# A planner that charges turns of the engines at a shared PSUM bank, with new durations for five kinds of work

## The chip, the cores and the metric

The kernel runs on one core of a Trainium2 chip. A core has five engines that run their own instruction streams: TensorE (PE) multiplies matrices and writes PSUM, VectorE (DVE) and ScalarE (ACT) work element by element, GpSimd (POOL) here issues indirect DMAs and does a few small vector steps, and SyncE (SP) issues the other DMAs. The metric is the device time in microseconds (us) of one execution; the median of three runs is compared. Times from the trace come from one profiled execution.

## The reference

Eight blocks of 512 tokens with 128 features (float32) pass through three layers, each added to its input:

```python
x = x + 0.5 * _L0_ffn_ref(_layernorm(x), ...)
x = x + _L0_attn_ref(_layernorm(x), ...)
x = x + 0.5 * _L0_ffn_ref(_layernorm(x), ...)
```

The feed-forward layer (FFN) normalizes each token, finds the nearest of 8 centroids, and sends the token through that expert alone: an up matrix of 128 x 512, `a * silu(g)` of its halves, and a down matrix of 256 x 128. The attention layer is a linear recurrence over the 512 tokens of a block. It projects r, k and v, takes sigmoid of r and exp of k, scans `kv` and `k` with a decay of its own for each channel, divides the two scans, multiplies by r, and projects with W_o.

## The kernel before

**Tables and pairs.** Tokens of one expert are brought together through tables in HBM. For each block, routing finds the expert and the slot of each token; ACT scales the rows (`xrow`, L442), and POOL scatters them with an indirect DMA into a table t (L706, 128 rows each, four for a block). Tiles of 128 slots are then gathered from the table by SP (`xg`, L856), with the weights of their expert (`wup`, L863). There are three tables: one for blocks 0 to 3 and one for blocks 4 to 7 in the first FFN, and one for all blocks in the second, which is filled in the batches (0,1), (2,3), (4,5), (6), (7). Unused slots of a table are filled with zeros by SP.

Two tiles make a pair; 44 pairs are numbered through: 0 to 11 and 12 to 23 in the first FFN, 24 to 43 in the second. A pair goes through these steps, in `pair`: transpose on PE into the x half of `ps_xy` (L869); copy to SBUF as `xgT`, mostly on ACT (L897); up, 16 passes on PE (L874); SILU on ACT into `sg` (L906); product on DVE (L911); down on PE into the y half of `ps_xy` (L882); `ys` on DVE, which adds the skip row (L918); and an indirect DMA for each tile on POOL that puts the rows back to the tokens' places (L924). `xg` holds seven pairs, `sg` three, `ys` four. Both halves of `ps_xy` are one PSUM bank. Another bank, `ps_small`, has scores of routing in one part ("d") and ranks in another ("r").

**Between the FFNs.** Attention works on the batches in turn: statistics (L470), a root on ACT and a newton step on POOL (L505 to L508), scaling and transposes, products for k, r and v on PE (L983), then `kv`, two scans and the divisions on DVE (L998 to L1010), and the output product on PE (L1033 to L1040). The results are the x of the second FFN, whose routing follows: statistics, roots, transposes (L517), scores (L612), nearest centroid (L629 to L663), ranks (L679 to L690), and places of tiles (L745 to L772). The first four pairs of the second FFN, 24 to 27, use tiles that are already full and are worked on beside attention.

**The order.** The steps are not issued as they are written. They are recorded as `Op`s in a `Plan`, with the buffers that each reads and writes (`Buf`), one or more ways (an engine, an estimated duration and a call), an order key by engine, and a lag. `schedule` is a list scheduler: it keeps for each engine when it is free, for each tag of buffers when a slot comes free, takes the op that could start first, and among those on the same engine that could start within `slack` the one with the lowest key. A release costs `HOP` = 0.1, an ACT table load `SWITCH` = 1.28. `trace` runs it with 48 settings of its three parameters and emits the calls in the order of the setting with the least planned span. Each engine then runs its own stream in that order, and waits by semaphores. The keys of a pair k on PE are `LATE + 10k - 13` for the transpose, `LATE + 10k` for up, and `LATE + 10k + 10` for down; the pair's steps on ACT and DVE go ahead of others (`FIRST + k`).

An op's buffer in `ps_xy` is a `Buf` with the tag "x" or "y", each with one slot. The schedule before knows nothing of two tags in one bank. The kernel as built, however, has waits between accesses to one bank by different engines.

Of the kernel before, what the change touches and what calls it, by code (L numbers as in the profile page):

```python
# [19 lines left out]
class Buf:  # L20


    def __init__(self, make, tag=None):
        self.make, self.tag, self.tile = make, tag, None
        self.writers, self.readers = [], []

    def __call__(self):
# [5 lines left out]
class Op:  # L33
    def __init__(self, ways, reads, writes, order, lag, table):
        self.ways, self.order, self.lag, self.table = ways, order, lag, table
        self.bufs = list(dict.fromkeys(list(reads) + list(writes)))
        self.needs, self.users = set(), []


class Plan:  # L40

# [13 lines left out]
    def add(self, ways, reads=(), writes=(), order=None, part=False, lag=0.0, table=None):  # L57
        op = Op(ways, reads, writes, order or {}, lag, table)
        for b in reads:
            op.needs.update(b.writers)  # L60
            b.readers.append(op)
        for b in writes:
            op.needs.update(b.readers)
            if not (part and not b.readers):
                op.needs.update(b.writers)
            if b.readers or not part:
                b.readers, b.writers = [], []
            b.writers.append(op)
        op.needs.discard(op)
        self.ops.append(op)  # L70

    def schedule(self, spare, wait, slack):

        left, ready, uses = {}, {}, {}
        for op in self.ops:
            left[op], ready[op] = len(op.needs), 0.0
            for b in op.bufs:
                uses[b] = uses.get(b, 0) + 1
        slots = {tag: [0.0] * n for tag, n in self.slots.items()}
        free, held, released, table = {}, set(), {}, None  # L80
        waiting = [op for op in self.ops if not op.needs]
        order, span = [], 0.0
        while waiting:
            could = []
            for op in waiting:
                at = ready[op]
                for b in op.bufs:
                    if b.tag and b not in held:
                        if not slots[b.tag]:
                            break  # L90
                        at = max(at, min(slots[b.tag]))
                else:
                    for n, (engine, cost, call) in enumerate(op.ways):
                        then = max(at, free.get(engine, 0.0))
                        if n == 0 or free.get(op.ways[0][0], 0.0) > then + spare:
                            if op.table not in (None, table):
                                then += wait
                            could.append((then, engine, cost, call, op))
            if not could:
                return None  # L100
            first = min(could, key=lambda c: c[0])
            start, engine, cost, call, op = min(
                (c for c in could if c[1] == first[1] and c[0] <= first[0] + slack),
                key=lambda c: (c[4].order.get(c[1], c[4].index), c[0]),
            )
            load = None
            if op.table not in (None, table):
                load = table = op.table
                cost += max(0.0, self.SWITCH - wait)
            order.append((op, call, load))  # L110
            for b in op.bufs:
                if b.tag and b not in held:
                    slots[b.tag].remove(min(slots[b.tag]))
                    held.add(b)
            waiting.remove(op)
            free[engine] = start + cost
            end = start + cost + op.lag
            span = max(span, end)
            for b in op.bufs:
                uses[b] -= 1  # L120
                released[b] = max(released.get(b, 0.0), end)
                if uses[b] == 0 and b.tag:
                    slots[b.tag].append(released[b] + self.HOP)
            for u in op.users:
                left[u] -= 1
                ready[u] = max(ready[u], end + self.HOP)
                if left[u] == 0:
                    waiting.append(u)
        return span, order
# [20 lines left out]
def kernel(  # L150
# [40 lines left out]
    P = 128  # L191
# [99 lines left out]
    ps_xy = ps_t.tile([P, 2 * (P + D)], F32, tag="xy", name="ps_xy")  # L291
# [13 lines left out]
    def part_of(bank, tag, at, width, count):  # L305

        slots[tag], n = count, [0]

        def make():
            first = at + n[0] % count * width  # L310
            n[0] += 1
            return bank[:, first : first + width]

        return lambda: Buf(make, tag)

    small_d = part_of(ps_small, "d", 0, TMAX * E, 128 // (TMAX * E))
    small_r = part_of(ps_small, "r", 128, E * (TMAX + 1), RBUF)
# [1 line left out]
    add = plan.add  # L319
    FIRST, LATE = -10**6, 10**6  # L320
    EXP, SILU = "natural_log_exp_and_others", "silu_and_others"
    x_ = [Buf(lambda b=b: xb[b]) for b in range(B)]
    wd_, wr_, wo_, routing_, attending_ = (Buf(lambda w=w: w) for w in (wsb, wrkv_sb, wo_sb, None, None))
# [139 lines left out]
    def moments(batch, n: str, mv):  # L463

        T = len(batch) * NT
        bn = buf(stat, [P, TMAX, 2, 3], F32, "bn", n, 4)

        def stats(i, b):
            for t in range(NT):
                nc.vector.bn_stats(  # L470
                    bn()[:, i * NT + t, :, :].rearrange("p a m -> p (a m)"), xb[b][:, t, :]
                )

        def aggregate():


            a, o = bn()[:, :T, 0, :], bn()[:, :T, 1, :]
            d = o[:, :, 0]
            nc.vector.tensor_tensor(
                mv()[:, :, :T].rearrange("p m t -> p t m"), a[:, :, 1:], o[:, :, 1:], ALU.add  # L480
            )
            nc.vector.tensor_sub(d, a[:, :, 1], o[:, :, 1])
            nc.vector.scalar_tensor_tensor(d, d, D / 4.0, d, ALU.mult, ALU.mult)
            nc.vector.tensor_add(mv()[:, 1, :T], mv()[:, 1, :T], d)

        for i, b in enumerate(batch):
            add([("DVE", 1.1, lambda i=i, b=b: stats(i, b))], [x_[b]], [bn], part=True)
        add([("DVE", 0.66, aggregate)], [bn], [mv, bn])

    def roots(n, va, rs, part, shape):  # L490
# [79 lines left out]
    def prepare(table, batch, near):  # L570

        f = table.f
        n = f"{f}_{batch[0]}"
# [30 lines left out]
        ps_d = small_d()  # L604
        rows = []
        for i, b in enumerate(batch):
            ps = side(f"x_{f}_{b}")
            xT = buf(work, [P, L], F32, "xT", f"{f}_{b}", 2)

            def products(i=i, xT=xT):  # L610
                for t in range(NT):
                    nc.tensor.matmul(  # L612
                        ps_d()[:, ts(i * NT + t, E)], xT()[:, ts(t, P)], cw, start=True, stop=True
                    )

            add([("PE", 0.5, lambda ps=ps, b=b: transposed(ps, x_[b]))], [x_[b]], [ps], lag=0.2)
            add(copied(xT, ps, L, 0.6, 0.68), [ps], [xT])
            add([("PE", 1.75, products)], [xT, routing_], [ps_d], lag=0.2, part=True)
            row = Buf(lambda b=b: xrow[b][:, :, :D])
            half = Buf(lambda b=b: xrow[b][:, :, D : 2 * D])  # L620
            at = i * NT
            add(scaled(x_[b], row, lambda at=at: rs()[:, 1, at : at + NT],
                       lambda at=at: nra()[:, 1, at : at + NT]), [x_[b], rs, nra], [row])
            add(scaled(x_[b], half, lambda at=at: one()[:, at : at + NT],
                       lambda at=at: nra()[:, 0, at : at + NT]), [x_[b], one, nra], [half])
            rows.append([row, half])
# [210 lines left out]
    def pair(k, table, parts, keep, spots, at_, downs, downs_, tiles):  # L837
        n = len(tiles)
        early = table.left > 0
        xg = buf(work, [P, 2, ROW], F32, "xg", k, 7)  # L840
        wup = buf(work, [P, 2, H2], F32, "wup", k, WUP)
        slots["x"] = slots["y"] = 1
        ps_x = Buf(lambda: ps_xy[:, : 2 * P], "x")
        xgT = buf(work, [P, 2 * P], F32, "xgT", k, 3)
        hp = buf(ps_t, [P, 2, H2], F32, "h", k, 2)
        sg = buf(work, [P, 2, H], F32, "sg", k, 3)
        ps_y = Buf(lambda: ps_xy[:, 2 * P :], "y")
        y = buf(work, [P, 2, D], F32, "ys", k, 4)
        soon = {"ACT": FIRST + k, "DVE": FIRST + k}

# [36 lines left out]
        for i, j in enumerate(tiles):  # L887
            add([("SP", 0.52, lambda i=i, j=j: rows(i, j))], [at_] + parts, [xg], {"SP": LATE + k},
                part=True, lag=2.3)
        for i, j in enumerate(tiles):  # L890
            add([("SP", 0.52, lambda i=i, j=j: weights(i, j))], [at_], [wup], {"SP": LATE + k},
                part=True, lag=3.8)
        add([("PE", 0.19 * n, features_first)], [xg], [ps_x],
            {"PE": LATE + 10 * k - 13}, lag=0.2)
        add(
            [
# [4 lines left out]
            ],  # L901
            [ps_x, cols_], [xgT], soon,
        )
        add([("PE", 0.95 * n, up)], [xgT, wup], [hp], {"PE": LATE + 10 * k}, lag=0.2)
        add(
            [("ACT", 0.16 + 0.22 * n, lambda: nc.scalar.activation(  # L906
                sg()[:, :n, :], hp()[:, :n, H:], AF.Silu))],
# [4 lines left out]
                sg()[:, :n, :], hp()[:, :n, :H], sg()[:, :n, :]))],  # L912
            [hp, sg], [sg], soon,
        )
        add([("PE", 0.53 * n, down)], [sg, downs_, wd_], [ps_y], {"PE": LATE + 10 * k + 10}, lag=0.2)

        half = lambda: ps_y()[:, : n * D].rearrange("p (i d) -> p i d", d=D)
        add([("DVE", 0.1 + 0.18 * n, lambda: nc.vector.scalar_tensor_tensor(  # L918
# [180 lines left out]
```

## Time and profile before

| | us |
|---|---|
| runs | 352.85, 346.55, 344.47; median 346.55 |
| profiled execution, its time | 316.78 |
| its span | 314.0 |
| PE busy | 231.9 (74%) |
| DVE busy | 179.6 (57%) |
| ACT busy | 163.1 (52%) |
| POOL busy | 177.2 (56%) |
| mean granted clock of PE | 0.899 |

Times in the trace count from the start of the span. In rows of instructions, `out<-in` gives the program's names of the tiles, followed by the number of instructions, busy time, mean duration in ns, and the idle time of the engine just ahead of them with what ended it. A wait "A <- B: total, times, longest" is idle time of A that ended when B did. Line numbers are those of the kernel before; in the kernel after, most lines are 8 further down.

### The profile page before, as it was taken

The page shows a single profiled execution, that of the slowest core. Times are in us where ns is not written, and L with a number is a line of the kernel's source. Part 1 is how long each engine was busy: PE and PEld are TensorE (multiplying, and loading weights), DVE is VectorE, ACT ScalarE, POOL GpSimd, SP SyncE. Part 2 cuts the span into 40 slices and gives each one's busy share as a digit, 9 for nine tenths or more (in the row PEclk, how much of TensorE's full clock was granted, in tenths as well). Part 3 has the DMA queues.
Part 4 walks back from the last instruction along what each step waited for, and adds up shares of the span by engine and source line. Part 5 has one row for each costly group of instructions (what it writes and reads, how often), then busy time and mean ns, then how long its engine had stood idle before and what let it go on. Part 6 is the DMA issues. An engine that isn't in the chain of part 4 may idle for free. (4 is left out here: it accounts for less than half of the span.)

```text
span 314.0 us, 5775 instructions
## 1 busy us (share of the span) xinstructions
PE 231.9 (74%) x1510; PEld 194.2 (62%) x1510; DVE 179.6 (57%) x604; ACT 163.1 (52%) x331; POOL 177.2 (56%) x258
## 2 busy tenths in 40 slices
PE   3747467789997889997969368799670186989980
PEld 2636356778897786766736222579470075989980
DVE  4677936314232474898888648999774703242340
ACT  3779951432332359983638565766875233324320
POOL 6268737777564475564446767015377623556663
PEclk9999999999999999997957559999965569999996
DMA  7912569998987996300024154520063488899810
GB/s 211 276 53 85 194 190 336 283 384 260 286 262 229 300 342 200 120 13 10 9 71 134 51 165 187 140 67 25 20 204 145 135 251 268 269 281 324 265 56 10
DMA packets 45138, 55.81 MB, mean 178 GB/s; under 512 B 6255, under 2 KB 31115, under 8 KB 45106
## 3 DMA queue, kind: packets, MB, share of 16 engines
q1 hardware_dynamic: 39286, 42.71, 45.3%
q0 software_dynamic: 5792, 12.73, 11.2%
q8 instruction: 12, 0.20, 0.3%
q14 instruction: 20, 0.16, 0.2%
q10 hardware_dynamic: 28, 0.01, 0.0%
HBM read 39.11 MB, written 17.68 MB: 181 GB/s over the span
## 5 line engine op out<-in xcount | busy, mean ns | idle before, releaser
L874 PE MATMUL h<-xgT,wup 128*128 128x128 f32 x680 | 87.9, 285 | 0.0
L874 PEld LDWEIGHTS h<-xgT,wup 128*128 128x128 f32 x680 | 84.6, 202 | 1.4 <-issue 1.4
L706 POOL DMA_INDIRECT t<-xrow,posi_t x64 | 65.1, 1017 | 30.3 <-issue 15.9
L924 POOL DMA_INDIRECT yt<-ys,xg x46 | 53.1, 1155 | 39.7 <-DVE ys L918 25.6
L924 POOL DMA_INDIRECT out_dram<-ys,xg x39 | 39.5, 1012 | 50.1 <-DVE ys L918 31.1
L911 DVE TENSOR_TENSOR sg<-h,sg 128x512 f32<-128x512 f32 (+1 forms) x44 | 29.1, 671 | 62.5 <-ACT sg L906 62.5
L882 PE MATMUL ps_xy<-wsb,sg 128*128 x340 | 48.2, 286 | 9.7 <-DVE sg L911 5.3
L897 ACT ACTIVATE xgT<-ps_xy,cols 128x256 f32<-128x256 f32 (+1 forms) x44 | 20.5, 465 | 61.2 <-DVE ys L918 33.5
L882 PEld LDWEIGHTS ps_xy<-wsb,sg 128*128 128x128 f32 x340 | 43.2, 198 | 12.8 <-ACT xgT L897 4.7
L906 ACT ACTIVATE sg<-h 128x512 f32<-128x512 f32 (+1 forms) x44 | 25.1, 582 | 37.3 <-PE h L874 37.2
L442 ACT ACTIVATE xrow<-x,nra,rs 128x128 f32<-128x128 f32 x64 | 26.3, 481 | 15.1 <-DVE nra L594 15.1
L612 PE MATMUL ps_small<-cw,xT 128*128 128x8 f32 x128 | 23.9, 319 | 11.4 <-ACT xT L459 6.5
L612 PEld LDWEIGHTS ps_small<-cw,xT 128*128 128x128 f32 x128 | 23.3, 275 | 14.0 <-ACT xT L459 12.7
L869 PE MATMUL ps_xy<-ident,xg 128*128 128x128 f32 x85 | 21.3, 308 | 13.4 <-DMA xg<-t 12.4
L918 DVE SCALAR_TENSOR_TENSOR ys<-ps_xy,xg 128x256 f32<-128x256 f32 (+1 forms) x44 | 18.1, 411 | 18.8 <-PE ps_xy L869 8.7
L442 ACT ACTIVATE xrow<-x,nra,one 128x128 f32<-128x128 f32 x64 | 26.1, 479 | 0.0
L869 PEld LDWEIGHTS ps_xy<-ident,xg 128*128 128x128 f32 x85 | 11.9, 150 | 20.2 <-DMA xg<-t 14.5
L144 ACT ACT_TABLE_LOAD x16 | 20.5, 1283 | 0.3
L679 PE MATMUL ps_small<-onehot_t,tri 128*128 128x32 f16 (+1 forms) x11 | 2.2, 196 | 20.0 <-DVE near L629 8.2
L470 DVE BATCH_NORM_STATS2 bn_f<-x 128x6 f32<-128x128 f32 x64 | 13.5, 277 | 4.3 <-DMA x<-in_L_attn_inputs_dram 3.8
L682 PEld LDWEIGHTS <-ones_h 128*128 128x128 f16 x11 | 1.1, 103 | 21.8 <-issue 21.8
L517 PE MATMUL side_x<-ident,x 128*128 128x128 f32 x64 | 13.1, 356 | 1.8 <-ACT x L459 1.4
(156 smaller groups left out, 319.1 us busy)
## 6 DMA issues: line engine op xcount, KB each, us to landing
wup<-in_L_ffn_up_w_dram SPq DMA_DIRECT2D x85, 256.0 KB
xg<-t SPq DMA_DIRECT2D x85, 130.0 KB
t<-fill SPq DMA_DIRECT2D x27, 130.0 KB
x<-in_L_attn_inputs_dram SPq DMA_DIRECT2D x8, 256.0 KB
x<-yt SPq DMA_DIRECT2D x8, 256.0 KB
wsb<-in_L_ffn_down_w_dram SPq DMA_DIRECT2D x8, 128.0 KB
t<-xrow,posi_t POOLq DMA_INDIRECT x64
yt<-ys,xg POOLq DMA_INDIRECT x46
```

Of the source, the lines that this page charges most:

```text
L144: self.load_table(load)
L442: nc.scalar.activation(out()[:, t, :], src()[:, t, :], AF.Identity, bias=bias()[:, t : t + 1], scale=scale()[:, t : t + 1],)
L612: nc.tensor.matmul(ps_d()[:, ts(i * NT + t, E)], xT()[:, ts(t, P)], cw, start=True, stop=True)
L706: ordered(table, nc.gpsimd.indirect_dma_start(out=table.at()[:, :], out_offset=bass.IndirectOffsetOnAxis(ap=posi()[:, q : q + 1], axis=0), ...
L869: nc.tensor.transpose(ps_x()[:, ts(i, P)], xg()[:, i, :D], ident)
L874: nc.tensor.matmul(hp()[:, i, ts(c, P)], wup()[:, i, ts(c, P)], xgT()[:, ts(i, P)], start=True, stop=True,)
L882: nc.tensor.matmul(ps_y()[:, ts(i, D)], sg()[:, i, ts(c, P)], wdown[c][:, ds(expert(downs[j]) * W, D)], start=(c == 0), stop=(c == NHC - 1),)
L897: ("ACT", 0.2 + 0.13 * n, lambda: nc.scalar.activation(xgT()[:, : n * P], ps_x()[:, : n * P], AF.Copy, scale=scale_c)),
L906: [("ACT", 0.16 + 0.22 * n, lambda: nc.scalar.activation(sg()[:, :n, :], hp()[:, :n, H:], AF.Silu))],
L911: [("DVE", 0.1 + 0.28 * n, lambda: nc.vector.tensor_mul(sg()[:, :n, :], hp()[:, :n, :H], sg()[:, :n, :]))],
L918: add([("DVE", 0.1 + 0.18 * n, lambda: nc.vector.scalar_tensor_tensor(y()[:, :n, :], half(), 0.5, xg()[:, :n, D : 2 * D], ALU.mult, ALU.ad ...
L924: inst = nc.gpsimd.indirect_dma_start(out=table.result()[:, :], out_offset=bass.IndirectOffsetOnAxis(ap=xg()[:, i, 2 * D : 2 * D + 1].bitc ...
```

## The change

A `Buf` may now name its bank: both parts of `ps_small` are in bank "small", both halves of `ps_xy` in bank "xy". For each bank, `schedule` keeps when each engine's last planned access ends, and starts an op on the bank no earlier than `HOP` after the end of every other engine's last access. Accesses by the same engine are not held. And five duration estimates are changed: statistics of one block on DVE 1.1 to 0.9, scores of one block on PE 1.75 to 1.5, the pair's transpose 0.19 to 0.17 a tile, up 0.95 to 0.9 a tile, down 0.53 to 0.5 a tile. The computation of each op is untouched.

```diff
-    def __init__(self, make, tag=None):
-        self.make, self.tag, self.tile = make, tag, None
+    def __init__(self, make, tag=None, bank=None):
+        self.make, self.tag, self.bank, self.tile = make, tag, bank, None
...
+        self.banks = {b.bank for b in self.bufs if b.bank}
...
                         then = max(at, free.get(engine, 0.0))
+                        for bank in op.banks:
+                            for other, end in banks.get(bank, {}).items():
+                                if other != engine:
+                                    then = max(then, end + self.HOP)
...
             end = start + cost + op.lag
+            for bank in op.banks:
+                banks.setdefault(bank, {})[engine] = end
...
-        return lambda: Buf(make, tag)
+        return lambda: Buf(make, tag, "small")
...
-            add([("DVE", 1.1, lambda i=i, b=b: stats(i, b))], [x_[b]], [bn], part=True)
+            add([("DVE", 0.9, lambda i=i, b=b: stats(i, b))], [x_[b]], [bn], part=True)
...
-            add([("PE", 1.75, products)], [xT, routing_], [ps_d], lag=0.2, part=True)
+            add([("PE", 1.5, products)], [xT, routing_], [ps_d], lag=0.2, part=True)
...
-        ps_x = Buf(lambda: ps_xy[:, : 2 * P], "x")
+        ps_x = Buf(lambda: ps_xy[:, : 2 * P], "x", "xy")
...
-        ps_y = Buf(lambda: ps_xy[:, 2 * P :], "y")
+        ps_y = Buf(lambda: ps_xy[:, 2 * P :], "y", "xy")
...
-        add([("PE", 0.19 * n, features_first)], [xg], [ps_x],
+        add([("PE", 0.17 * n, features_first)], [xg], [ps_x],
...
-        add([("PE", 0.95 * n, up)], [xgT, wup], [hp], {"PE": LATE + 10 * k}, lag=0.2)
+        add([("PE", 0.9 * n, up)], [xgT, wup], [hp], {"PE": LATE + 10 * k}, lag=0.2)
...
-        add([("PE", 0.53 * n, down)], [sg, downs_, wd_], [ps_y], {"PE": LATE + 10 * k + 10}, lag=0.2)
+        add([("PE", 0.5 * n, down)], [sg, downs_, wd_], [ps_y], {"PE": LATE + 10 * k + 10}, lag=0.2)
```

More of the change, by code (lines that the diff above doesn't have):

```diff
@@ L79, in schedule @@
         slots = {tag: [0.0] * n for tag, n in self.slots.items()}
-        free, held, released, table = {}, set(), {}, None
+        free, held, released, table, banks = {}, set(), {}, None, {}
         waiting = [op for op in self.ops if not op.needs]
```

## The prediction

> **What bounds the kernel now.** I read the page's rows and slices first, then the list of waits, then timelines of the stretches where the order moves most. No engine is full, and the limit changes by stage:
>
> ```profile
> PE   3747467789997889997969368799670186989980
> PEclk9999999999999999997957559999965569999996
> DMA  7912569998987996300024154520063488899810
> ```
>
> Each digit is a fortieth of 314.0 us, 7.85 us. Slices 8 to 15 (60 to 117 us) are pairs of the first FFN: PE and DMA both near full. Slices 33 to 39 are the last pairs. Between them DMA is nearly idle, and PE drops to half clock around 229.8 to 257.1 us: there the kernel waits for a chain that goes through several engines. That chain is where an order can cost or gain.
>
> The waits show where PSUM turns already stand:
>
> ```profile
> ACT xgT L897 <- DVE ys L918: 33.5, 23, 4.1
> POOL out_dram L924 <- DVE ys L918: 31.1, 10, 15.6
> SPq L856 <- DMA t<-xrow,posi_t: 23.3, 6, 10.7
> ```
>
> Columns: total us, times, longest us. The first is the turn that the change charges: the x half of the pair bank is read by ACT only after DVE has read the y half, although the halves are different buffers. Each such wait (mean 33.5/23 = 1.46 us) is on ACT while PE is in its 16 passes, so most cost nothing: a steady pair takes about 3.36 us, PE needs 0.38 + 1.95 + 1.06 = 3.39 minus overlaps (about 2.9), and DMA is 0.94 busy in 60 to 117 us. The other two rows are the gap before pair 28: POOL idle for 15.6 us until ys of pair 24, and SP waiting 10.7 us for scatters. The timeline of POOL in it:
>
> ```profile
> 211.06 1.19 POOL L924 DMA_INDIRECT out_dram<-ys,xg  x1 [15.64 <-DVE ys L918]
> 216.54 1.39 POOL L924 DMA_INDIRECT out_dram<-ys,xg  x1 [2.99 <-DVE va L588]
> 225.35 1.01 POOL L924 DMA_INDIRECT out_dram<-ys,xg  x1 [4.56 <-DVE slot_t L690]
> 227.95 0.97 POOL L706 DMA_INDIRECT t<-xrow,posi_t  x1 [0.30 <-ACT x L459]
> 243.82 0.96 POOL L706 DMA_INDIRECT t<-xrow,posi_t  x1 [1.06 <-ACT xrow L442]
> 245.09 0.96 POOL L706 DMA_INDIRECT t<-xrow,posi_t  x1 [0.30 <-ACT xrow L442]
> ```
>
> From 225.35 POOL is full, a DMA each 1.27 us (0.97 and 0.30 of issue). SP gathers xg_28 only when the first two scatters of xrow_6 (started 243.82 and 245.09) have landed: it issues at 247.65, 2.56 after the second starts. Then:
>
> ```profile
> 249.95 1.05 PE L869 MATMUL ps_xy<-ident,xg 128*128 128x128 f32 x2 [3.58 <-DMA xg<-t]
> 253.34 3.62 PE L874 MATMUL h<-xgT,wup 128*128 128x128 f32 x16
> ```
>
> So from the last step of attention on batches 4 and 5 (num_4 final on DVE, ends 205.54; call it N4) POOL's queue sets when the 16 last pairs start, 42.1 us later.
>
> **What the change does to the work.** No instruction's arithmetic changes. The new durations lie by their rows: bn_stats, four of 0.21, 0.86 against 0.9; products 23.9/16 = 1.49 against 1.5; transposes 0.38 for two tiles against 0.34; up 1.8 between starts against 1.8; down 1.06 against 1.0. They and the bank turns only choose another order. Three things differ in count: ACT table loads 16 to 18, one copy (xT_0_7) goes from ACT to DVE, one scaling of batch 7 from DVE to ACT as four instructions. I follow the built order of both through the stages, placing each instruction by the durations of its row.
>
> *Start to the first pair (0 to 50 us).* Two rank matmuls of the first table go ahead of later products and places for its tiles come about 1.6 us earlier; but nra_0_4 falls behind on DVE, so the rows of blocks 4 to 7 are scaled to about 48.5 instead of 43.95, and PE's registers for the second table are read ahead of UP of pair 1. Between -3 (all the earlier places) and +2; I take -0.5, because the gather waits for scatters on POOL, whose number is unchanged.
>
> *First FFN (50 to 117 us).* The same pattern (transpose k+1, UP k, down k-1) to pair 12. Then in three places UP and down are two pairs apart, each with a turn of the bank ahead of it of 1.1 to 1.2 us. Against it, the layer-norm statistics of batch 0, which stop DVE for 3.25 us until the block is loaded (and PE for 1.59 + 0.73 behind it), come a pair later: up to -2. With DMA at 0.94, 0, from -2 to +2.
>
> *Attention of batches 0 to 3 with pairs 19 to 23 (117 to 164 us).* The last five pairs now come ahead of the key/receptance/value products of these batches. DVE binds it (33.1 of 40 us busy in 117 to 157); no operation is added, but attention's DVE work starts later by the pairs put before it: +1 by what the places of their DVE instructions move, +3.6 if all of it shows. The earlier loads of blocks 4 to 7 help only a stage that is not bound by them. I take +1.5.
>
> *To N4 (164 to 205 us).* The scaling and keys of batches 4 and 5 go ahead of the row scaling of blocks 2 and 3 on ACT (6.26 us of it in one run), and two newtons ahead of scatters on POOL; but er_4 stays behind these rows, and the two side banks then hold up the value product. From -2.5 to +1.5; I take -0.5. N4 comes +0.5 later.
>
> *N4 to the gather of pair 28.* This is the step that decides. In the order before, on PE down of pair 24 comes ahead of the output product of batch 6; after, behind it and behind the transposes of batch 6. On DVE ys_24 has nine instructions after N4 ahead of it before (4.8 us: 205.54 to 210.36). After, it is behind three scans, the rest of batches 6 and 7, all statistics of batches 4 to 6 and the whole nearest-centroid chain to onehot8_t2_4. By rows: 5 of 0.68 and 3 of 0.75 (L1005), 3 scans of 1.22, 2 sg of 0.67, kv 0.65, statistics 3 x 0.86 and 8 x 0.17, va, nra and one 0.8, near and argmin 1.76: 17.8, and 0.5 for a wait on the scores' matmuls: ys_24 starts at N4 + 18.3. Out scatters of pair 24 stand at the head of POOL's queue, as before, and start 0.7 after ys_24 does: N4 + 19.0 in place of N4 + 5.5. In front of xrow_6's second scatter stand then 2 + 3 + 1 + 1 + 2 + 1 + 2 + 1 + 3 + 1 = 17 DMAs and two newtons (1.1 each by the rows of 237.79 on): it starts at N4 + 19.0 + 17 x 1.27 + 2.2 = N4 + 42.8, and with 2.56 to the issue xg_28 is at N4 + 45.4, against 42.1 before: +3.3, and 0.2 for what POOL still waits on its way (8.6 in three waits before). Between +0 (DVE gets there earlier, because parts of batches 6 and 7 are done before N4) and +8 (the scatters also wait for rows of 6 and 7, whose scaling ACT does late). I take +3.5, the sum by rows.
>
> Queued behind are also the two new table loads, on ACT around sg_26, sg_27 and the roots of batches 6 and 7. The row:
>
> ```profile
> L144 ACT ACT_TABLE_LOAD x16 | 20.5, 1283 | 0.3
> ```
>
> The Trainium skill's "ScalarE: Activation LUTs", section "What ACT_TABLE_LOAD costs", says that a switch is 1283 ns and about 1380 of drain, 2.66 in all. The row has 1283, but idle of 0.3 for all 16 together, and the first instruction after the load starts 0.01 later: no drain shows here. By the row the two are 2 x 1.283 = 2.6 us, by the page 5.3. At POOL's pace of 17 DMAs behind them, 2.6 is covered; 5.3 would put roots of 7 behind their scatter and show about 1. I take 0, between 0 and +2.6.
>
> *Pairs 28 to 43 (254 to 314 us).* The SILU table is loaded right after the second pair's xgT instead of after the third's, so sg of pair 28 follows its UP at once: before, PE waited 1.74 us. Against it xg_30's second tile is behind zero fills on SP, xg_31 behind weights that wait for UP of 28. From -2 to +1; I take -0.5.
>
> The "PSUM — Partial Sum Buffer" page of the same skill, section "PSUM bank collisions raise a hardware error", speaks for a charge: two engines may not touch one bank in the same part at once, whatever the address. The 33.5 us row is what a program pays for that. By the rule, 23 turns are worth up to 33.5 us if avoided; by the row they lie under UP, and the pair stage's PE idle for them is L882 behind ACT and DVE, 6.8 + 4.6 us in all of the run, most outside 60 to 104. I therefore count no general gain.
>
> **Sum.** -0.5 + 0 + 1.5 - 0.5 + 3.5 + 0 - 0.5 = +3.5; the clock adds 0.5 if one more transpose falls at half speed (0.48 against 0.19 a tile), so +4. On the profiled execution: 316.78 (314.0 span and 2.78 around it) + 4 = 320.8. The median of the runs shown is 346.55, 29.8 above that execution, and the page doesn't say where those lie; I add the 4 as such: 350.55, said 350.5.
>
> **Rivals.**
> *Faster.* The pairs and attention take the cover away from three stalls: 3.25 (statistics of batch 0), 3.58 (DVE for the value product at 125.05), 1.28 (the load at 257.86), in all 8.1, and DVE reaches ys_24 early enough that POOL is not later. 346.5 - 8.1 = 338.4. For it: all three are gone from their place. Against: DVE binds there, and POOL's gap is 15.64 already.
> *Same.* The stages are bound by DMA and by busy DVE, which do not change; the turns were paid by both orders, so the new charge only reshuffles: 346.5, within 2 either way. It is also the case that the change doesn't do what it says. For it: every total of work is unchanged. Against: ys_24's place.
> *Slower by over 2%.* The one mechanism is the late ys_24 at POOL's head: with attention's +3.6 and pushing scatters to the +8 bound, 346.5 + 11.5 = 358. It decides from about 7 us more in the gap. For it: POOL is in order and full afterwards; its cover (8.6 us of waits before) is used up.
>
> **Chances.** Forecast (+1.5 to +7) 0.50, the same 0.15, slower 0.25, faster 0.10. 2% is 6.9 us, and the three runs before spread 344.47 to 352.85, so that is about what can be told from no change. Part of the forecast, near its top, may read over the bound: slower 0.29, same 0.61, faster 0.10. The range that leaves out 2 in 10 goes from 342 to 360.
>
> **What would show it.** In the trace after: POOL idle in one piece of over 20 us before the first out_dram scatter of the second half, ys_24 some 18 us after N4, no idle on POOL behind it, and xg_28 issued 45 to 46 us after N4; N4 itself within 3 us of 205.5; 18 table loads and their idle still near 0.3; steady pairs at 3.3 to 3.4. The prediction is wrong if N4 moves by more than 4 us, or if PE's waits for bank turns in 60 to 117 us fall by more than 3.

## The result, and the profile after

The kernel after took 360.51 us (median of 4 runs, 356.21 to 361.15) where the kernel before, measured with it, took 347.27 (344.47 to 352.85). The ratio is 1.035, 95% interval 1.029 to 1.041. It is slower by more than 2%; the prediction had 350.5 and gave that case 0.29. A ratio leaves out the runs that are over 1.5% above the fastest of the same kernel, and a median takes all runs, so the two can differ.

The two kernels took 347 and 361 us in this first measurement and 321 and 327 us in all later ones, on four chips; the pages don't show why, and the chip of the first is not known. The profile of before that the prediction was read from (316.78) fits the later level, and the profile of after from the first measurement (361.15, span 359.4) does not. So I compare traces and medians within like conditions: before (314.0, and 320.0 for a second trace) against the kernel after run again (325.2 and 325.8).

The slices of the page of after, first measurement, in the same rows as before (a slice is 9.0 us):

```profile
PE   3568206777885879797939765599772177967880
PEclk9999555599999889999867877879685578999996
DMA  8723657787767698410400153420252558877610
```

The half-clock stretch around the gather of pair 28 is there again (slices 30 and 31 counted from 0, 270 to 288 us; the gather is at 280.93), and there is another in slices 4 to 7, 36 to 72 us, up to the first ys at 71.61. Work in total is nearly the same: 1510 matmuls, 604 instructions on VectorE, 258 on GpSimd, and 336 in place of 331 on ScalarE. The table loads of the same page:

```profile
L152 ACT ACT_TABLE_LOAD x18 | 23.1, 1283 | 0.3
```

18 of the same 1283 ns with 0.3 of idle in all, as the prediction took them: no drain shows. The waits that answer to those shown of before, from the trace of after run again (325.2):

```profile
ACT xgT L905 <- DVE ys L926: 7.0, 5, 2.5
POOL tr L513 <- ACT yr L505: 34.0, 2, 20.0
SPq L864 <- DMA t<-xrow,posi_t: 24.5, 8, 12.9
```

The bank's turns, ACT's xgT behind DVE's ys, fall from 33.5 us to 7.0. The order pays fewer turns; the time went elsewhere. (The charge is not what removes them: with the new durations and no charge, in the run dur_only below, this wait is 6.5 us, and with the charge and the old durations, in bank_only, 26.1.) GpSimd's longest wait is now 20.0 us, for the roots of batches 4 and 5 in the routing of the second FFN. And there is a part of GpSimd's timeline (first measurement) that no row shown of before resembles:

```profile
211.03 2.31 POOL L714 DMA_INDIRECT t<-xrow,posi_t  x1 [0.30 <-issue]
213.36 1.11 POOL L513 TENSOR_TENSOR tr_a<-van,yr_a 128x4 f32<-128x4 f32 x1
214.54 2.06 POOL L514 TENSOR_TENSOR tr_a<-tr_a,yr_a 128x4 f32<-128x4 f32 x1
216.69 1.10 POOL L515 TENSOR_TENSOR tr_a<-three_halves,tr_a 128x4 f32<-128x4 f32 x1
217.87 1.11 POOL L516 TENSOR_TENSOR rn<-tr_a,yr_a 128x4 f32<-128x4 f32 x1
219.13 1.00 POOL L714 DMA_INDIRECT t<-xrow,posi_t  x1 [0.15 <-issue]
```

This is the newton step of batch 7 in attention: 4 small instructions on 128 x 4 numbers, 5.6 us from start to end. In a trace of before the same four take 1.1. The columns are start, duration, engine, line, operation. Beside it, VectorE in the same trace:

```profile
213.13 1.28 DVE L1013 SCALAR_TENSOR_TENSOR den<-kT,gam,den 128x1024 f32<-128x1024 f32 x1
214.33 2.28 DVE L1018 TENSOR_TENSOR_SCAN num<-lam_l,kv 128x1024 f32<-128x1024 f32 x1
216.53 1.20 DVE L1013 SCALAR_TENSOR_TENSOR den<-den,er 128x1024 f32<-128x1024 f32 x1
217.65 1.28 DVE L1013 SCALAR_TENSOR_TENSOR num<-kv,gam,num 128x1024 f32<-128x1024 f32 x1
```

VectorE's four end at 214.41, 216.61, 217.73 and 218.93; GpSimd's four end at 214.47, 216.60, 217.79 and 218.98. Each of GpSimd's instructions ends with one of VectorE's. The profile that the prediction was read from has the same on a smaller scale: a newton step of 0.55 us, where the others take 0.20, beside an instruction of VectorE that ends 0.05 us before it:

```profile
176.71 0.55 POOL L507 TENSOR_TENSOR tr_a<-three_halves,tr_a 128x4 f32<-128x4 f32 x1
176.53 0.68 DVE L966 TENSOR_TENSOR xl<-x,rn 128x512 f32<-128x512 f32 x1
```

And ScalarE waits for what they make (first measurement again):

```profile
213.01 0.59 ACT L467 COPY xlT<-side_xl 128x512 f32<-128x512 f32 x1 [0.60 <-PE side_xl L525]
219.01 1.27 ACT L980 ACTIVATE xl<-x,rn 128x128 f32<-128x128 f32 x4 [5.42 <-POOL rn L516]
220.20 0.67 ACT L999 ACTIVATE kT<-side_k,acols 128x512 f32<-128x512 f32 x1
```

That xl of batch 7 is the scaling that the change moved from VectorE to ScalarE. It now holds ScalarE for 5.42 us, with keys of batch 6 and the reciprocals of batches 4 and 5 queued behind it. GpSimd's queue did not bring the step late: it starts at 213.36, and ScalarE comes free at 213.60.

### The profile page after: what moved, and what is told of

Its sections match the earlier page's. It is cut to its first block, busy times and chain, and to the rows that moved or that the text cites. A ratio compares the mean times of both kernels' runs of the same rounds, so it can differ in the third digit from the quotient of the medians.

```text
span 359.4 us, 5761 instructions
## 1 busy us (share of the span) xinstructions
PE 244.8 (68%) x1510; PEld 201.7 (56%) x1510; DVE 181.1 (50%) x604; ACT 165.4 (46%) x336; POOL 176.8 (49%) x258
## 5 line engine op out<-in xcount | busy, mean ns | idle before, releaser
L882 PE MATMUL h<-xgT,wup 128*128 128x128 f32 x680 | 94.0, 298 | 5.6 <-ACT xgT L905 5.0
L882 PEld LDWEIGHTS h<-xgT,wup 128*128 128x128 f32 x680 | 90.0, 213 | 6.7 <-ACT xgT L905 5.7
L714 POOL DMA_INDIRECT t<-xrow,posi_t x64 | 64.3, 1005 | 37.6 <-issue 19.6
L932 POOL DMA_INDIRECT yt<-ys,xg x46 | 48.2, 1048 | 53.4 <-DVE ys L926 36.7
L919 DVE TENSOR_TENSOR sg<-h,sg 128x512 f32<-128x512 f32 (+1 forms) x44 | 29.5, 669 | 81.3 <-ACT sg L914 61.6
L932 POOL DMA_INDIRECT out_dram<-ys,xg x39 | 38.5, 987 | 45.3 <-DVE ys L926 30.4
L890 PE MATMUL ps_xy<-wsb,sg 128*128 x340 | 49.3, 290 | 12.4 <-DVE ys L926 12.4
L890 PEld LDWEIGHTS ps_xy<-wsb,sg 128*128 128x128 f32 x340 | 44.5, 203 | 16.9 <-DVE ys L926 14.9
L450 ACT ACTIVATE xrow<-x,nra,one 128x128 f32<-128x128 f32 x64 | 26.1, 480 | 0.0
L620 PEld LDWEIGHTS ps_small<-cw,xT 128*128 128x128 f32 x128 | 21.3, 255 | 5.7 <-issue 2.8
L620 PE MATMUL ps_small<-cw,xT 128*128 128x8 f32 x128 | 21.6, 301 | 2.9 <-issue 1.9
L152 ACT ACT_TABLE_LOAD x18 | 23.1, 1283 | 0.3
L513 POOL TENSOR_TENSOR tr<-va,yr 128x8 f32<-128x8 f32 (+1 forms) x11 | 2.8, 256 | 37.6 <-ACT yr L505 33.3
L1048 PEld LDWEIGHTS side_o<-wo_sb,num 128*128 128x128 f32 x64 | 10.6, 237 | 10.4 <-DVE num L1013 6.5
```

Of the source, the lines that this page charges most:

```text
L152: self.load_table(load)
L450: nc.scalar.activation(out()[:, t, :], src()[:, t, :], AF.Identity, bias=bias()[:, t : t + 1], scale=scale()[:, t : t + 1],)
L620: nc.tensor.matmul(ps_d()[:, ts(i * NT + t, E)], xT()[:, ts(t, P)], cw, start=True, stop=True)
L714: ordered(table, nc.gpsimd.indirect_dma_start(out=table.at()[:, :], out_offset=bass.IndirectOffsetOnAxis(ap=posi()[:, q : q + 1], axis=0), ...
L882: nc.tensor.matmul(hp()[:, i, ts(c, P)], wup()[:, i, ts(c, P)], xgT()[:, ts(i, P)], start=True, stop=True,)
L890: nc.tensor.matmul(ps_y()[:, ts(i, D)], sg()[:, i, ts(c, P)], wdown[c][:, ds(expert(downs[j]) * W, D)], start=(c == 0), stop=(c == NHC - 1),)
```

## Where the time went, stage by stage

From the traces in like conditions (means of two: before 314.0 and 320.0, after 325.2 and 325.8), worked out from the starts of instructions; N4 is the end of the last division of batches 4 and 5:

| stage | before | after | difference | forecast |
|---|---|---|---|---|
| start to ys of pair 0 | 60.6 | 60.8 | +0.2 | -0.5 |
| to the last division of batches 2 and 3 | 101.2 | 107.2 | +6.0 | +1.5 |
| to N4 | 44.1 | 42.5 | -1.6 | -0.5 |
| N4 to the gather of pair 28 | 44.7 | 48.9 | +4.3 | +3.5 |
| gather to ys of pair 28 | 14.8 | 12.9 | -1.9 | -0.5 with the next |
| to ys of pair 43, and the end | 51.7 | 53.2 | +1.5 | |

The forecast's remaining +0.5 is its term for the clock, which it gave to no stage. The sum is +8.5 between spans; the medians say +6.0 and +5.7. Two traces of one kernel differ by up to 5.1 us in a row (before, N4 to the gather: 42.1 and 47.2), so a row alone proves little.

Pairs 19 to 23 end 11 us earlier (ys of pair 23 at 147.9 against 158.9), as their place in the order foretold, and attention of blocks 0 to 3 pays it back: the first scatter of the second FFN starts at 174.8 and 176.3 against 166.4 and 168.0, and pair 24 is gathered at 208.2 and 209.3 against 197.2 and 200.2.

## The experiments

My first theory was the prediction's: ys of pair 24 late, at the head of GpSimd's queue, so the gap before pair 28 is longer. All kernels below do the same operations in another order, some of them on another engine. Times are medians; both kernels spread by 3 to 4% within a measurement, so I read medians taken together against each other and give the ratio with its interval beside them. The edits are shown in part; `...` stands for lines left out, and a comment for the lines that do what it says.

**A second trace of before.**

```diff
(no edit)
```

> The kernel before, unedited, for a second trace. Its profiled execution took 316.78 us where its timed runs took 344 to 353, while the kernel after took 361.15 in its profiled execution and 356 to 361 in its timed runs: the two traces at hand may not be alike. If the 30 us are in the execution and not in the kernel, a new profile reads 340 to 352 us, and has stalls that the first lacks: a first ys near 70 us instead of 59.7, and pairs of 4 us instead of 3.4. If the first profile is the rule for a profiled execution, it reads 314 to 320 again, and then the kernel after lost 45 us by its order alone.

321.97 us, span 320.0. The first profile of before was no oddity: under these conditions the kernel takes about 320, timed (321.03) or profiled. Neither case of the expectation was quite met (314 to 320, or 340 to 352). The second is the nearer in its number, but what it concluded, a loss of 45 us by the order, does not follow: the 30 us lie in the conditions of the first measurement. What they consist of the pages don't show.

**The kernel after in these conditions.**

```diff
(no edit)
```

> The kernel after, unedited, in the conditions in which the kernel before has its profile near 316 to 322 us. Theory (the order itself costs the 3.5%): 1.03 to 1.04 times the kernel before, near 332 us, with its trace later than before's by some 4 us at the first pair and 4 to 8 us in the gap before pair 28. Rival (the loss belongs to the conditions of the first measurement, in which gathers and completions came late, and this order only bears them worse): within 1% of the kernel before, near 321 us.

326.61 against 320.6; ratio 1.018, interval 1.003 to 1.033. Between the two cases. The loss is the order's own, but 6 us here and 13 in the first measurement; the two intervals just touch. What makes it larger in the first stays open, as there is no trace of before at that level. A later measurement, with six runs of after, gave 326.76 against 321.02 without a ratio:

> The kernel after's order, unedited, beside the three others in the same call: ratio to the kernel before 1.01 to 1.035, as the two measurements so far (1.018 and 1.035) leave it. If it comes at 1.03 while the conditions are those of the 320 us of before, the loss is the order's; if at 1.018 or less, the first measurement's surplus belongs to its conditions.

The same 1.8%, by medians.

**Parts of the change.** The durations alone, the charge alone, and the new durations with the charge for one bank:

```diff
 dur_only:   -  return lambda: Buf(make, tag, "small")    +  return lambda: Buf(make, tag)
             -  ps_x = Buf(..., "x", "xy"), ps_y alike    +  ps_x = Buf(..., "x"), ps_y alike
 bank_only:     the five durations as before
 xy_only:    -  return lambda: Buf(make, tag, "small")    +  return lambda: Buf(make, tag)
 small_only: -  ps_x = Buf(..., "x", "xy"), ps_y alike    +  ps_x = Buf(..., "x"), ps_y alike
```

> The five new durations, and no charge for a bank. Theory (it is the charge that puts the steps of pairs 24 to 27 behind attention): within 2% of the kernel before, 341 to 353 us. Rival (any change of the planner's numbers reshuffles the order of all stages, and the order before was a lucky one): 354 to 366 us, like the kernel after.

> The charge for turns at a bank, with the five old durations. Theory (the charge is the cause): 354 to 366 us, like the kernel after, with ys of pair 24 more than 12 us behind the last division of batches 4 and 5. Rival (the durations, or the reshuffle as such): anywhere from 341 to 366, with ys of pair 24 within 8 us of that division if it is as fast as before.

> New durations, and the charge at the pair bank alone (x and y halves of ps_xy), not at the routing bank. Theory (the pair bank's charge holds down of pair 24 back): 354 to 362 us, ys of pair 24 late. Rival (the routing bank's charge, which orders scores and ranks, is what moves the starts of the FFNs): within 2% of before, 341 to 353 us.

> New durations, and the charge at the routing bank alone. Theory (both charges together are what puts pair 24's steps behind attention): near the kernel before, 314 to 322 us, ys of pair 24 within 8 us of the last division of batches 4 and 5. Rival (the routing bank's charge alone does it): 328 us or more, ys of pair 24 more than 12 us behind.

| kernel | us | before, measured with it | ratio |
|---|---|---|---|
| dur_only | 312.87 | 321.03 | 0.989 (0.983 to 0.995) |
| bank_only | 319.81 | 321.03 | none taken |
| xy_only | 317.12 | 321.03 | 1.001 (0.995 to 1.007) |
| small_only | 319.38 (one run) | 320.6 | none taken |

The first, second and third expectation gave their times at the level of the first measurement, where before took 347. No part is slower, as far as one run can say it of small_only. The charge with the old durations has ys of pair 24 14.7 us behind N4, as the theory wanted, and still takes 319.81: the first blow to the theory. xy_only was expected as slow as after by the theory and is level; small_only has ys of pair 24 10.3 us behind N4, between its theory's 8 and its rival's 12. Neither the charge nor the durations is the cause; only the one order that both together choose is slow. dur_only is the fastest kernel of the study, 1.1% under before by the ratio.

**Which side of N4.** In one kernel the planner makes both orders, and they are joined at the last division of batches 4 and 5:

```diff
+        after = best()
+        ... banks cleared, old durations ...
+        before = best()
+        cut = next(i for i, (op, _) in enumerate(first) if op.name == ("attended", 4)) + 1
+        order = first[:cut] + [e for e in then if e[0] not in done]
         # ab_n4: first = after, then = before;   ba_n4: first = before, then = after
```

> A joined order: the kernel after's up to the last division of batches 4 and 5, and what is left in the kernel before's order. Theory (some 2 us are lost before that division and 4 to 5 behind it): about 2 us over the kernel before, ratio 1.003 to 1.01. Rival (the loss comes from attention of all batches being put behind pairs 19 to 23): 5 us or more over it, ratio over 1.014.

> The other joined order: the kernel before's up to the last division of batches 4 and 5, then the kernel after's. Theory: 3 to 5 us over the kernel before, ratio 1.009 to 1.016, with ys of pair 24 more than 15 us behind the division and xg of pair 28 about 49 us behind it. Rival (as above): within 1.5 us of the kernel before.

Beside them before took 321.02, and after's whole order, made by the same code, 326.76. ab_n4: 329.48, ratio 1.037 (1.029 to 1.045). ba_n4: 322.17, ratio 1.018 (1.011 to 1.024). The theory had it the other way round: after's order ahead of N4 brings at least the whole loss, and the intervals of the two don't overlap. What its order behind N4 costs is not settled: 1.2 us by the medians, which is the rival's case, and 1.8% by the ratio, which is more than the theory's. By the medians the two losses add up to 9.7 us where after has 5.7, so a joined order has costs of its own.

The traces say more. ba_n4 has ys of pair 24 16.7 us behind N4, yet gathers pair 28 at N4 + 44.2, where before has ys at 4.8 and 9.9 and gathers at 42.1 and 47.2. From ys of pair 24 to the gather it is 27.5 us in ba_n4, 27.5 and 27.6 in the two of after, and 37.3 in both of before: the new order sends late, but has ten us less behind the first send. So late sends as such cost next to nothing here. What is longer in after is the way to ys of pair 24, N4 + 22.0 and 20.8 in place of 16.7, with the same instructions ahead of it on VectorE (15.7 us busy, 15.5 in ba_n4). The rest is VectorE's waiting, of which the longest piece (3.6 and 2.1 us) is for x of block 4, and this leads to pair 24, transposed at 210.4 and 211.5 in place of 199.3 and 202.2. First after (325.2), then ba_n4:

```profile
210.43 1.09 PE L877 MATMUL ps_xy<-ident,xg 128*128 128x128 f32 x2 [3.22 <-DMA xg<-t]
213.85 1.91 PE L1048 MATMUL side_o<-wo_sb,num 128*128 128x128 f32 x8
```

```profile
210.00 1.05 PE L1071 MATMUL side_o<-wo_sb,num 128*128 128x128 f32 x8
```

PE stands 3.22 us for the late gather of pair 24, ahead of the output product of block 4, and that product then takes 1.91 us at a granted clock of 0.50 (mean of 210 to 215 us); in ba_n4 it takes 1.05 at 1.00.

**The sends moved forward.**

```diff
+        for k in range(24, 28):
+            steps = [e for e in order if e[0].name in (("down", k), ("ys", k), ("send", k))]
+            # down right behind the pair's product, ys and sends two DVE instructions later
```

> The kernel after, with one thing moved in its finished order: down, ys and sends of pairs 24 to 27 stand right behind their products (down at once, ys two DVE instructions later) instead of behind attention's and routing's steps. Theory (the late ys of pair 24 at the head of GpSimd's queue makes the gap before pair 28 longer): xg of pair 28 issues 3 to 5 us sooner after the last division of batches 4 and 5 than the 49.5 of the unedited order, and the run is 3 to 5 us under the unedited kernel after in this call. Rival (the scatters of the last rows wait for ACT and DVE anyway, so that earlier sends only leave GpSimd idle at another place): within 1.5 us of the unedited kernel after, with new idle times on GpSimd among the scatters of blocks 5 to 7.

331.21 us, ratio 1.045 (1.038 to 1.052): 4.4 us over after, not 3 to 5 under it. GpSimd's timeline in this kernel:

```profile
221.63 0.99 POOL L943 DMA_INDIRECT out_dram<-ys,xg  x1 [17.20 <-DVE bn_f L498]
227.35 1.18 POOL L943 DMA_INDIRECT out_dram<-ys,xg  x1 [3.43 <-DVE ys L936]
236.90 1.01 POOL L722 DMA_INDIRECT t<-xrow,posi_t  x1 [5.93 <-ACT xrow L458]
249.40 0.98 POOL L943 DMA_INDIRECT out_dram<-ys,xg  x1 [3.03 <-DVE cum_t L686]
```

The sends go out sooner (from N4 + 12.8, in place of 22.8 and 21.5) and GpSimd then idles among the scatters, 5.93 us for rows from ScalarE: the expectation's rival in kind, though it had expected no more than 1.5 us either way. The gather of pair 28 is at N4 + 54.4. The first theory is dropped: earlier sends don't bring the gather forward.

**The second theory: two steps ahead of N4.** The traces of after showed two delays in scattering blocks 0 to 3: ranks of the first batch stand behind the output product of block 3 on PE (one-hot ready at 169.10, ranks at 172.99, in the trace of 325.2), and the newton step of batch 7 that takes 4.8 to 5.6 us.

```diff
 rank:
+        for name in (("ranks", "t2_0"), ("places", "t2_0")):   # to behind what they need
 rank_newton, besides:
+        at = next(i for i, e in enumerate(order) if e[0].name == ("newton", "a7"))
+        order[at] = (order[at][0], order[at][0].ways[1][2], order[at][2])   # its DVE way
```

> The same with the ranks and places alone; the newton step of batch 7 stays on GpSimd. Theory: pair 24 gathered some 3.5 us sooner than in the kernel after (near 205 us), half of the gain, 2 to 3 us. If the newton step's long instructions (1.1 and 2.06 us where others take 0.22) come from VectorE's scans beside it, they stand there again, at a place that has moved with them. Rival: no gain over the kernel after, within 1 us.

> The kernel after with two steps moved in its finished order: ranks of the first batch of the second FFN (and the places that follow from them) ahead of the output product of block 3, and the newton step of batch 7 from GpSimd to VectorE at the same place in the order. Theory, formed from the traces so far (both hold back the scatters of blocks 0 to 3, so that pair 24 is gathered 10 us late): the last scatter of block 3 starts near 197 us instead of 205, xg of pair 24 is issued near 200 us instead of 208 to 209, and the run is 4 to 6 us under the kernel after, within 1% of the kernel before. Rival (pair 24 comes late because attention of all batches is late, or its lateness is covered): under 1.5 us gained, with pair 24 gathered early or not.

rank: 327.48, ratio 1.025 (1.019 to 1.031); rank_newton: 321.86, ratio 1.008 (1.005 to 1.011), before 320.59 in both. The ranks alone win nothing, as the rival had it. The first scatter starts earlier (172.3), and then GpSimd waits for the roots of attention, next in its queue:

```profile
172.29 1.01 POOL L725 DMA_INDIRECT t<-xrow,posi_t  x1 [6.21 <-issue]
175.65 0.20 POOL L521 TENSOR_TENSOR tr_a<-van,yr_a 128x8 f32<-128x8 f32 x1 [2.35 <-ACT yr_a L513]
```

The newton step, moved to VectorE, takes 5.6 us off, of the 6.9 that rank is over before (1.7 of 2.5% by the ratios). In rank it still stands on GpSimd, long as ever, and ScalarE behind it; in rank_newton ScalarE doesn't wait there. First rank, then rank_newton:

```profile
192.22 0.59 ACT L475 COPY xlT<-side_xl 128x512 f32<-128x512 f32 x1 [0.43 <-PE side_xl L534]
198.46 1.28 ACT L995 ACTIVATE xl<-x,rn 128x128 f32<-128x128 f32 x4 [5.65 <-POOL rn L524]
202.47 0.75 DVE L1021 SCALAR_TENSOR_TENSOR kv<-side_v,acols,kT 128x512 f32<-128x512 f32 x1 [4.11 <-PE side_v L1006]
```

```profile
194.99 0.58 ACT L477 COPY xlT<-side_xl 128x512 f32<-128x512 f32 x1 [0.47 <-PE side_xl L536]
195.48 1.28 ACT L997 ACTIVATE xl<-x,rn 128x128 f32<-128x128 f32 x4
201.71 0.74 DVE L1023 SCALAR_TENSOR_TENSOR kv<-side_v,acols,kT 128x512 f32<-128x512 f32 x1
```

The last row of each shows how it reaches N4: keys of batch 6 come behind ScalarE's wait and the values behind the keys, and VectorE stands 4.11 us for the values in rank and not at all in rank_newton. From ys of pair 23 to N4 it is 59.0 us in rank_newton and 62.7 in rank, and from N4 to the gather of pair 28 46.9 and 48.4: 3.7 + 1.4 = 5.1, against 5.6 by the medians. The expectation's path was wrong in part: it looked for the gain at the gather of pair 24 (206.2, only 2.1 us earlier than in rank); most of it goes through ScalarE, to N4.

The other traces agree. From the last division of batches 2 and 3 to N4 it takes 41.7 to 43.3 us in all six traces in which this newton step lasts 4.8 to 5.6 us (three of after, ab_n4, early, rank), and 37.6 to 39.2 in dur_only, bank_only, xy_only, small_only and rank_newton, where it lasts 1.5 us or less. (In before's order, which arranges this stretch otherwise, it takes 43.6 to 44.6.) The newton step alone, with the ranks left in their place, was not run.

In the second trace of before the same step falls where VectorE is idle:

```profile
187.02 0.21 POOL L505 TENSOR_TENSOR tr_a<-van,yr_a 128x4 f32<-128x4 f32 x1
187.31 0.20 POOL L506 TENSOR_TENSOR tr_a<-tr_a,yr_a 128x4 f32<-128x4 f32 x1
187.59 0.20 POOL L507 TENSOR_TENSOR tr_a<-three_halves,tr_a 128x4 f32<-128x4 f32 x1
187.87 0.20 POOL L508 TENSOR_TENSOR rn<-tr_a,yr_a 128x4 f32<-128x4 f32 x1
```

## Why the prediction was right or wrong

*Size and sign.* +4 was forecast, +6 measured in the conditions of the profile that the sum was made on, and +13 in the first measurement. The sign was right. "Within 2%" was given 0.61, and failed. 360.51 lies half a us above the stated range (342 to 360), and 1.035 times 346.55, 358.7, just inside it; that the range holds so nearly is luck, as half of the 13 us belongs to conditions that nobody foresaw. That the median lay 29.8 above the profile and "the page doesn't say where" was the weak place: a loss read from a quick execution was carried over as such.

*Start to the first pair; first FFN.* -0.5 and 0. Measured +0.2 in the first, and from ys of pair 0 to ys of pair 12 45.2 against 41.5, which pairs 13 to 18 give back (-0.3 at ys of pair 18). Right over the whole of each stage.

*Attention of batches 0 to 3.* +1.5 forecast, with +3.6 "if all of it shows". Measured from ys of pair 18 to the last division of batches 2 and 3: +6.3. This term was mis-sized. The prediction had VectorE bind this stage (33.1 of 40 us busy in 117 to 157); in the two traces of after VectorE is busy 29.5 and 28.8 there. That attention comes behind pairs 19 to 23 was seen; what its lateness is made of was not tested apart. It is not the whole loss: rank_newton is no earlier at this point (170.4, in after 167.5 and 168.6) and within 1% of before at the end.

*To N4.* This is the step that failed in its mechanism, although its number holds: -0.5 forecast, -1.6 measured. The -0.5 named "two newtons ahead of scatters on POOL" as a gain and did not look at the third, batch 7's, which the new order puts beside VectorE's scans. "One scaling of batch 7 from DVE to ACT" was listed as a difference in count and costed at nothing. Together they are the 3.92 and 5.76 us (5.42 in the first measurement) that ScalarE waits. Without them the stage would have made up for most of the late attention; rank_newton, 38.3 us in place of rank's 43.1, shows it.

*N4 to the gather of pair 28.* +3.5 forecast, +4.3 measured. The queue's arithmetic holds: 17 DMAs and two newtons were put at 23.8 us, and from the first send to xrow_6's second scatter it took 24.1 in the trace of 325.2; from ys of pair 24 to the gather the forecast's 27.1 stands beside 27.5 and 27.6. The way to ys of pair 24 was put at 18.3, of which 17.8 busy on VectorE and 0.5 waiting. It is 15.7 busy and 6.3 and 5.1 waiting: the wait is the term that was mis-sized, and its longest piece goes back to pair 24's late gather, ahead of N4. With the old order ahead of N4 and the same one behind it, ys is at N4 + 16.7 and the gather at N4 + 44.2, no later than before.

*Table loads.* 0, between 0 and +2.6. Both are there, at 1283 ns, with no idle before them. That they are covered was argued, not tested.

*From the gather of pair 28.* -0.5 forecast, -1.9 + 1.5 = -0.4 measured. I have no cause for the +1.5 in the last pairs.

*The signs.* Of those named, these came: over 20 us of idle on GpSimd ahead of the first send (20.0, and 3.9 more behind the roots), next to none behind it, 18 table loads with 0.3 of idle. These did not: ys of pair 24 some 18 us behind N4 (22.0 and 20.8), the gather at 45 to 46 (49.5 and 48.4), steady pairs at 3.3 to 3.4 (3.6 and 3.9 from pair 0 to 12, where before has 3.4 and 3.5), N4 within 3 us of 205.5 (209.2 and 211.9). One trace of the two moves N4 by more than the 4 us at which the prediction called itself wrong. PE's waits for bank turns in 60 to 117 us fell from 1.9 and 3.2 us to 0 and 0.5, by the means less than the 3 us of the other such sign.

*The rivals.* "Slower" came true by sign; of its two terms, attention's came in full and more (+6.3 where it had 3.6), and the +8 in the gap did not. "Same" holds for every single part of the change: the charge for either bank and the durations alone are no slower than before. "Faster" is what the durations alone bring, 1.1%; not for the change as it was.

*What stays open.* Why the first measurement is 8 and 10% slower for the two kernels (another chip is one candidate), and why after loses 13 us there; what makes attention of batches 0 to 3 late; what the order behind N4 costs; and the last 0.8% that rank_newton still lacks.

## What to carry to other kernels

A planner's better model is not a better order: four neighbours of this change were level or faster and the change itself was slower, for the most part because one small step landed beside the wrong neighbour. Before trusting a new order, list the few instructions that changed engine or crossed another queue's long instructions, and look at who waits on them; totals don't show it. Four tiny vector steps on GpSimd are cheap only where no long instruction of VectorE runs beside them: their price is that of VectorE's instructions beside them.

## What the runs showed of the hardware

GpSimd's small vector instruction takes 0.20 us alone and 1.1 to 2.06 beside VectorE's scans and scalar-tensor-tensor instructions on 128 x 1024 float32, and ends within 0.1 us of one of them, in the traces of after, after run again, rank, and both kernels that start with after's order (ab_n4 and early). Of the 892 instructions of newton steps in the fourteen traces 101 take over 0.4 us, and each of these ends within 0.1 us of such an instruction of VectorE or of a product or scaling of 0.4 us or more. The Trainium skill's "SBUF — State Buffer", section "SBUF: two separate sides", says that the two engines share a pair of ports by an exclusive lock, taken for a whole instruction where VectorE has two SBUF inputs and GpSimd reads SBUF. The rows agree with it. An estimate from that rule and the rows: four steps, each held until one of VectorE's instructions of 1.2 to 2.28 us ends, are 5 to 6 us in place of 1.1. Set beside that rule, the newton step would have had a price of some 4.5 us in the prediction instead of nothing. Scatters beside these instructions took 1.5 to 3.0 us in place of 0.96 as well, in before too; whether by the same lock no run here tells.
